# Spreading the last routing over the expert pairs and reordering the step from attention to experts, in a gated cross-attention and mixture-of-experts kernel

## The chip, the cores and the metric

The kernel runs on one core of a Trainium2 chip. The core has a matrix engine (TensorE, PE in the profile, with its weight loads shown as PEld), VectorE (DVE), ScalarE (ACT), GpSimd (POOL) and SyncE (SP), which here issues most of the DMA transfers. Each engine has its own instruction stream and takes it in order; semaphores tie the streams together. The metric is the device time of one execution in microseconds (us).

## The reference

All arithmetic is in fp32. There are 32 sequences of 112 tokens of width 256, each with a context of 375 rows. First, 16-head cross-attention from the normalized tokens to context and tokens together, with a gated residual; then a mixture of 8 experts of width 1024 with the best two chosen for each token, again with a gated residual.

```python
def _L0_xattn_ref(x, latents, ...):          # x: context, latents: tokens
    x, lat = layer_norm(x, ...), layer_norm(latents, ...)
    q = lat @ Wq
    k, v = split(concatenate([x, lat], axis=1) @ Wkv)
    attn = softmax(einsum('bhid,bhjd->bhij', q, k) * scale)
    return (attn @ v) @ Wout

def _L0_ffn_ref(x, gate_w, w1, b1, w2, b2):
    gate_scores = softmax(xf @ gate_w)
    topk_scores, topk_idx = top_k(gate_scores, 2)     # then normalized to sum 1
    h = gelu(einsum('td,edf->etf', xf, w1) + b1[:, None, :])
    y = einsum('etf,efd->etd', h, w2) + b2[:, None, :]
    out = sum over the two experts of topk_scores * y[expert, token]

x = x + tanh(g_xattn) * _L0_xattn_ref(ctx, _layernorm(x), ...)
x = x + tanh(g_ffn) * _L0_ffn_ref(_layernorm(x), ...)
```

The kernel does not compute all experts for all tokens: it sorts token rows by expert into a table in DRAM and computes only the chosen ones.

## The kernel before

The order of the work on each of the five engines is written out by hand: the order in which the program calls its helpers is the order of each engine's stream (`manual_schedule`). A helper call appends to several streams at once.

**Attention** is a loop of `LAST` = 128 steps n. A step handles four heads of one sequence. Its softmax is pipelined: in step n, VectorE transposes step n's weights in blocks of 32 (`turn_blocks`), SyncE sends them to DRAM in four transfers (`send_blocks`) and takes them back in another layout as `exT` (`take_blocks`, 1 MB, in slot h = 1); TensorE computes step n+1's `scores`, VectorE their maxima, ScalarE the exponentials (`exps`), VectorE a reciprocal and ScalarE a scaling by it (`norm`, in slots 1 and 3). `attend(j)` multiplies the weights of steps 2j and 2j+1 with the values; it is called in step 2j+3, and attend(63) stands behind the loop. A step has five slots h = 0 to 4; the lists `slots` and `pe` hold TensorE work for each slot, `dve` work for other engines, `after` transfers issued in slot 1 behind take_blocks. `ps_m` is a ring of four PSUM tiles that nearly all TensorE results go through, so each result needs the tile of four results earlier to have been read.

**Routing.** Every 128 tokens form a slab: `project`, `residual` (which stores the slab to the output and takes its statistics), `normed`, `gate_turn` and `gate_scores`. Slabs are routed in groups (six of four slabs, then slabs 24 and 25, then 26 and 27) by 13 parts r[0] to r[12] of `route_parts`: largest, equal, first, rest, largest, equal, first, apart, counts, places (two TensorE products), gates, slots_of, out_to. The last part puts two scatters per slab into `outgoing`; a scatter is an indirect DMA from GpSimd that writes one slab's rows to one expert each. `locate_early` and `locate_late` then work out from the counts (`counted`, one TensorE product) where each pair of blocks lies; the latter is cut in 11 pieces by its `yield`s.

**Experts.** There are 21 pairs t = 0 to 20 of 2 x 128 rows of one expert, the first 13 (`EARLY`) located after 20 slabs and the other 8 (`LATE`) after all. Pair 0 is computed plainly between the last attention steps (`hidden_plain`, one hidden chunk of 128 at a time, and `second_plain`). Each later pair uses seven products per layer where eight would be plain (`hidden_pair`, `second_pair`), with sums by VectorE and GpSimd. In the loop, iteration t runs hidden_pair(t), fetches pair t+1's first weights (`fetch_first`: a bias and seven transfers; for many pairs they are skipped on the chip when the expert stays the same), turns pair t+1's rows (`turn_rows`, `rows_sums`), does a few pieces of routing from the list `todo`, runs second_pair(t-1), adds its rows to the output from GpSimd (`out_pair`), fetches the second weights (`fetch_second`) and the rows of pair t+3 (`fetch_rows`). Every fetch_rows waits on all scatters issued since the one before (`behind_all`). Expert weights of the first and second layer have one buffer each. Behind the 21 pairs come single blocks (`run`).

Three places that the change and the steps of the prediction touch:

- the list `todo` (from L1627): what is left of the routing of slabs 24 and 25 (counts, places, gates, slots_of, out_to), then that of slabs 26 and 27, then the 11 pieces of locate_late: 38 entries, two of them empty, done six per iteration from t = 1 by `pieces_of(6)`;
- the iteration with t + AHEAD == EARLY, that is t = 10, in which the rest of `todo` and all of `outgoing` are done ahead of fetch_rows(13), the first fetch that needs the late table;
- steps 125 to 127 (`LAST - 3` to `LAST - 1`), where the expert work starts, and the calls between the loop and iteration t = 1.

Of the kernel before, what the change touches and what calls it, by code (L numbers as in the profile page):

```python
# [10 lines left out]
AF = mybir.ActivationFunctionType  # L11
ALU = mybir.AluOpType
# [11 lines left out]
def kernel(  # L24
# [152 lines left out]
    if True:  # L177
# [331 lines left out]
        def norm(n, p):  # L509
            b, i = heads_of(n)[0], heads_of(n)[1][p]  # L510
            rc = soft.tile([P, 2], F32, tag="rc", name=f"rc_{b}_{i}", bufs=4)
            nc.vector.reciprocal(rc, sm.pop((b, i)))  # L512
            for j in range(2):
                t = exs[n % 2][:, :, p, :, j, :]
                nc.scalar.mul(t, t, rc[:, j : j + 1])  # L515

        def turn_blocks(n, p):

# [90 lines left out]
        def normed(i, eng=nc.gpsimd):  # L609
            g, j = group[i]  # L610
            eng.tensor_scalar(
                xr[g][:, j, 0, :D], x1[i], mvx[i][:, 0, 0:1], rsx[i], ALU.subtract, ALU.mult
            )
            soon_.append(lambda: nc.gpsimd.tensor_copy(xr[g][:, j, 1, :D], xr[g][:, j, 0, :D]))
# [291 lines left out]
        def locate_late():  # L906

            has, behind_ = rank, macc  # L910
            nc.vector.tensor_scalar(has, found["ps"], float(P), None, ALU.is_ge)
            nc.vector.tensor_tensor(behind_, found["ps"], eoff, ALU.add)
            nc.vector.scalar_tensor_tensor(behind_, behind_, float(-PADS), has, ALU.add, ALU.mult)
            nc.vector.tensor_scalar(behind_, behind_, float(PADS), None, ALU.add)
            found["behind"] = mp.tile([P, E], I32, name="behindi")
            nc.vector.tensor_copy(found["behind"], behind_)
            yield
            rest = mp.tile([P, E], F32, name="restl")
            nc.vector.tensor_tensor(rest, found.pop("ps"), found["taken"], ALU.subtract)
            full, first = whole_blocks("b", rest, None, 0.0, 2 * P)  # L920
            yield
            taken = taken_of("b", first, full, LATE)
            start = mp.tile([P, E], F32, name="startl")
            nc.vector.tensor_tensor(start, found["start"], taken, ALU.add)
            yield
            yield from located("b", first, found["start"], row2, 2 * P, False)
            yield
            _, first = whole_blocks("c", rest, taken, float(P - 1), P)
            yield
            yield from located("c", first, start, row, P, True)  # L930
            yield
# [139 lines left out]
        def hidden_plain(lo, hi):  # L1071
            if lo == 0:
                hid[0] = found["tiles"].tile([P, NF, 2, P], F32, tag="h", name="h_0")
            for f in range(lo, hi):
                ps = ps_m.tile([P, 2, P], F32, tag="m", name=f"ps_h_0_{f}")
                for k in range(KD):
                    nc.tensor.matmul(
                        ps,
                        lhsT=found["w1"][:, k, f * P : (f + 1) * P],
                        rhs=xsT[0][:, k],  # L1080
                        start=(k == 0),
                        stop=(k == KD - 1),
                    )
                nc.scalar.activation(  # L1084
                    hid[0][:, f], ps, AF.Gelu, bias=bias[0][0][:, f : f + 1]
                )

        def second_plain(b):
            banks.append(banks.pop(0))
            ps = psy[0, b] = banks[-1][:, 0, :D]  # L1090
            for f in range(NF):
                nc.tensor.matmul(
                    ps,
                    lhsT=hid[0][:, f, b, :],
                    rhs=found["w2"][:, f, :],
                    start=(f == 0),
                    stop=(f == NF - 1),
                )

        def add_rows(t, b, y):  # L1100
# [26 lines left out]
                add_rows(t, b, y[:, b])  # L1127


        def hidden_pair(t):  # L1130


            h = hid[t] = found["tiles"].tile([P, NF, 2, P], F32, tag="h", name=f"h_{t}")
            x, v = xsT[t], xt[t]
            H = NF // 2
            h11, h12, h21, h22 = (h[:, i : i + H, b, :] for i in (0, H) for b in range(2))

            def product(n, w, r):
                ps = ps_m.tile([P, H, P], F32, tag="m", name=f"ps_h_{t}_{n}")
                for c in range(H):  # L1140
                    nc.tensor.matmul(
                        ps[:, c, :], lhsT=wt[w][:, c * P : (c + 1) * P], rhs=r, start=True, stop=True
                    )
                return ps

            def gelu(lo):
                for f in range(lo, lo + H):
                    nc.scalar.activation(h[:, f], h[:, f], AF.Gelu, bias=bias[t][0][:, f : f + 1])  # L1148

            add = nc.vector.tensor_tensor  # L1150
            nc.scalar.copy(h11, product(1, "11", x[:, 0, 0]))
            add(h12, product(6, "s2", v[:, 1]), h11, ALU.add)
            add(h21, product(7, "s3", v[:, 2]), h12, ALU.add)
            ps = product(5, "s1", v[:, 0])
            add(h22, ps, h21, ALU.add)
            add(h12, ps, h12, ALU.add)
            add(h21, product(4, "22", v[:, 3]), h21, ALU.add)  # L1157
            gelu(H)
            add(h11, product(2, "12", x[:, 1, 0]), h11, ALU.add)
            add(h12, product(3, "s4", x[:, 1, 1]), h12, ALU.add)  # L1160
            gelu(0)

# [293 lines left out]
        for n in range(LAST):  # L1456
# [121 lines left out]
                found["early"] = ctx.enter_context(tc.tile_pool(name="early", bufs=1, side="right"))  # L1578
                after += [lambda: fetch_rows(0), weights_ahead]
            if n == LAST - 3:  # L1580
                pe[4].append(lambda: turn_rows(0, nc.scalar.copy))
            if n == LAST - 2:

                pe[0].append(lambda: others(ends))
                after.append(lambda: fetch_first(1))
                for h in range(1, 5):
                    pe[h].append(lambda h=h: hidden_plain(h - 1, h))
            if n == LAST - 1:
                after += [lambda: fetch_second(1)]
                after += [lambda t=t: fetch_rows(t) for t in range(2, 1 + AHEAD)]  # L1590
                for h in range(4):
                    pe[h].append(lambda h=h: hidden_plain(h + 4, h + 5))
                pe[4].append(lambda: turn_rows(1))

            if n > 1 and n % 2:
# [1 line left out]
            more = n + 1 < LAST  # L1597
            if more:
                scores(n + 1)
                exps(n + 1, 0)  # L1600
            for h in range(5):
                for unit in slots[h] + pe[h]:
                    unit()
                if h == 4:
                    break
                if h == 1:
                    take_blocks(n)
                    do(after)
                if more and h in (1, 3):
                    norm(n + 1, h // 2)  # L1610
                if more and h == 3:
                    turn_blocks(n + 1, 0)
                then_ = soon_[:]
                del soon_[:]
                do(then_)
                for part in dve[h]:
                    part()

                if outgoing and (h % 2 == 0 or n > LAST - NG):
                    outgoing.pop(0)()  # L1620
                if extra:
                    do(extra.pop(0))
                if more and h == 0:
                    exps(n + 1, 1)


# [1 line left out]
        r, _ = route_parts(g, nc.vector)  # L1628

        todo = [[part] for parts in extra for part in parts]  # L1630
        todo += [[lambda j=j: normed(j, nc.vector), now] for j in (i, i + 1)]
        todo += [[]]
        todo += [[lambda p=p, j=j: p(j)] for j in (i, i + 1) for p in (gate_turn, gate_scores)]
        todo += [[part] for part in r[:9]] + [[]] + [[r[9]]]
        todo.append([lambda: found.update(ps=counted())])
        todo += [[part] for part in r[10:]]
        late = locate_late()
        todo += [[lambda: next(late)]] * 11

        def pieces_of(n):  # L1640
            for _ in range(min(n, len(todo))):
                do(todo.pop(0))
# [2 lines left out]
        for b in range(2):  # L1645
            second_plain(b)
        rows_sums(1)
        hidden_pair(1)
        attend(LAST // 2 - 1)
        for u in range(2):  # L1650
            project(i + u)
# [3 lines left out]
        for t in range(1, PAIRS):  # L1655
            if t > 1:
                hidden_pair(t)
            fetch_first(t + 1)
            turn_rows(t + 1, nc.scalar.copy if t > 1 else None)
            if t + 1 < PAIRS:  # L1660
                rows_sums(t + 1)
            pieces_of(6)
            hidden_sums(t)
            if t > 1:
                second_pair(t - 1)
# [3 lines left out]
                combine(0)  # L1669
                do(found.pop("sums"))  # L1670
            if t + AHEAD == EARLY:
                pieces_of(len(todo))
                do(outgoing)
                del outgoing[:]
            fetch_rows(t + AHEAD)
# [70 lines left out]
```

## Time and profile before

| | |
|---|---|
| three runs | 2023.91, 2027.59 and 2034.03 us, median 2027.59 |
| profiled execution, timed | 2025.86 us |
| its span, first to last instruction | 2024.2 us |
| mean granted TensorE clock | 0.994 |

| stretch of the span, us | TensorE busy | VectorE busy | GpSimd busy | granted clock | DMA share |
|---|---|---|---|---|---|
| 0 to 1540 | 1504.55 | 1134.95 | 743.70 | 1.00 | 0.74 |
| 1540 to 1600 | 50.99 | 23.71 | 14.30 | 0.94 | 0.73 |
| 1600 to 1711 | 100.03 | 78.36 | 78.02 | 0.94 | 0.63 |
| 1711 to 1890 | 174.73 | 91.61 | 129.19 | 1.00 | 0.85 |
| 1890 to 2024 | 122.20 | 19.60 | 29.35 | 0.98 | 0.61 |

The first stretch is attention up to step 123, the second the passage to the experts, the third pairs 2 to 8, the fourth pairs 9 to 20, the last the single blocks. Rows of the timeline merge neighbouring instructions of one line; a row gives the start, the time up to the last one's end, the engine, the line, the operation with output and inputs, the count, and in brackets the idle time of the engine before it with what ended it. `SPq` is SyncE's queue of DMA issues: its durations are those of issuing, not of the transfer. Granted clock is the share of full speed at which TensorE was allowed to run; it is 1.0 or 0.5 at any moment.

### The profile page before, as it was taken

Reading aid. Unit: us, or ns where it says so; the run is one execution under the profiler, and the core shown is the slowest. Engines: PE = TensorE matmul, PEld = TensorE weight load, DVE = VectorE, ACT = ScalarE, POOL = GpSimd, SP = SyncE. Lnnn points to the kernel's source line nnn. Section 1 sums busy time; section 2 is a strip of 40 time slices with the busy share of each in tenths; the row PEclk is TensorE's granted clock in tenths of the full one; section 3 lists DMA queues with packets and bytes.
Section 4 is the critical chain, followed back from the end, with each engine's and each line's share of the span. In section 5 each row is a group of like instructions: output and inputs, shape, how many; then the busy total and the mean of one; then the engine's idle time right before and its main releaser. Section 6 shows DMA issues by size and latency. Waiting matters only on the chain. (4 is left out here: it accounts for less than half of the span.)

```text
span 2024.2 us, 41138 instructions
## 1 busy us (share of the span) xinstructions
PE 1952.5 (96%) x14352; PEld 1494.6 (74%) x14352; DVE 1348.2 (67%) x2417; ACT 1156.5 (57%) x2718; POOL 994.6 (49%) x1469
## 2 busy tenths in 40 slices
PE   8999999999999999999999999999998899999998
PEld 4676767676667677767666676777676799999887
DVE  6777776777786767676777777777776467545111
ACT  5666666656666666566666666666656233334342
POOL 5534243435265745564556555642424367767322
PEclk9999999999999999999999999999999899999999
DMA  7676666667677878788878778876657567799773
GB/s 218 199 224 191 180 193 185 197 167 208 197 233 221 260 216 245 220 262 232 258 211 260 220 239 231 255 222 175 190 166 240 185 194 202 197 324 285 204 210 51
DMA packets 261057, 433.40 MB, mean 214 GB/s; under 512 B 30729, under 2 KB 149073, under 8 KB 244465
## 3 DMA queue, kind: packets, MB, share of 16 engines
q1 hardware_dynamic: 248384, 414.37, 68.6%
q0 software_dynamic: 11328, 15.33, 3.9%
q8 instruction: 115, 1.88, 0.4%
q10 hardware_dynamic: 1136, 1.05, 0.2%
q14 instruction: 94, 0.76, 0.1%
HBM read 301.37 MB, written 172.28 MB: 234 GB/s over the span
## 5 line engine op out<-in xcount | busy, mean ns | idle before, releaser
L501 ACT ACTIVATE ex<-bank,nmx 128x512 f32<-128x512 f32 x512 | 348.7, 689 | 259.7 <-DVE nmx L492 259.7
L515 ACT ACTIVATE ex<-ex,rc 128x512 f32<-128x512 f32 x512 | 342.4, 720 | 202.8 <-DVE rc L512 201.5
L492 DVE TENSOR_REDUCE nmx<-bank 128x2 f32<-128x974 f32 x256 | 286.2, 1158 | 122.6 <-PE bank L482 122.6
L520 DVE STREAM_TRANSPOSE ex<-ex 128x1024 f32<-128x1024 f32 x256 | 315.1, 1231 | 28.4 <-ACT ex L515 25.6
L422 POOL TENSOR_TENSOR kT<-tmpk,kT 128x487 f32<-128x487 f32 x63 | 76.9, 1221 | 388.1 <-ACT kT L440 388.1
L412 PEld LDWEIGHTS ps_v<-wkv_s,tT 128*128 128x128 f32 x1536 | 189.3, 192 | 77.7 <-DVE kT L446 35.7
L482 PE MATMUL bank<-kT,qTs 64*128 64x487 f32 x1024 | 243.7, 594 | 0.0
L546 PE MATMUL ps_o<-exT,vv 128*64 128x112 f32 (+1 forms) x4096 | 211.2, 260 | 1.5 <-ACT h L1084 1.5
L412 PE MATMUL ps_v<-wkv_s,tT 128*128 128x128 f32 x1536 | 199.0, 278 | 11.6 <-DVE kT L446 10.0
L546 PEld LDWEIGHTS ps_o<-exT,vv 128*64 128x64 f32 (+1 forms) x4096 | 197.4, 136 | 9.5 <-ACT h L1084 1.9
L446 DVE TENSOR_TENSOR vv<-ps_v,vv 128x512 f32<-128x512 f32 x192 | 131.9, 687 | 108.4 <-PE ps_v L412 85.9
L406 PE MATMUL ps_k<-tT,wkv_s 128*128 128x487 f32 x378 | 181.0, 583 | 13.9 <-DVE vv L446 13.8
L412 PEld LDWEIGHTS ps_v<-wkv,kvT 128*128 128x128 f32 x1024 | 129.2, 191 | 72.4 <-issue 65.5
L1102 POOL DMA_INDIRECT out_dram<-y,xs x60 | 93.4, 1557 | 168.0 <-DVE y L1126 79.3
L422 POOL TENSOR_TENSOR vv<-tmpv,vv 128x512 f32<-128x512 f32 x64 | 81.5, 1274 | 190.7 <-ACT vv L440 190.6
L482 PEld LDWEIGHTS bank<-kT,qTs 64*128 64x128 f32 x1024 | 88.1, 186 | 103.3 <-issue 92.4
L1330 POOL TENSOR_TENSOR piece<-piece 128x128 f32<-128x128 f32 x256 | 117.3, 458 | 61.5 <-DMA piece<-in_L_ffn_w_dram 41.1
L446 DVE TENSOR_TENSOR kT<-ps_k,kT 128x487 f32<-128x487 f32 x189 | 123.3, 657 | 29.5 <-PE ps_k L406 24.3
L412 PE MATMUL ps_v<-wkv,kvT 128*128 128x128 f32 x1024 | 141.4, 281 | 0.0
L406 PE MATMUL ps_k<-kvT,wkv 128*128 128x487 f32 x252 | 130.2, 598 | 0.0
L333 PE MATMUL ps_q<-kvT,wq_sb 128*128 128x224 f32 x512 | 120.0, 356 | 1.4 <-ACT kvT L321 0.7
L1148 ACT ACTIVATE h<-h,b 128x256 f32<-128x256 f32 x160 | 66.2, 495 | 93.4 <-DVE h L1157 92.8
(297 smaller groups left out, 3683.4 us busy)
## 6 DMA issues: line engine op xcount, KB each, us to landing
turned<-ex SPq DMA_DIRECT2D x512, 256.0 KB
exT<-turned SPq DMA_DIRECT2D x128, 1024.0 KB
w<-in_L_ffn_w_dram SPq DMA_DIRECT2D x132, 256.0 KB
w_s<-ws SPq DMA_DIRECT2D x80, 256.0 KB
w_t<-ws SPq DMA_DIRECT2D x80, 256.0 KB
w_b2x<-in_L_ffn_w_dram SPq DMA_DIRECT2D x38, 512.0 KB
ws<-piece SPq DMA_DIRECT2D x64, 256.0 KB
cin<-in_ctx_dram SPq DMA_DIRECT2D x32, 336.0 KB
```

Of the source, the lines that this page charges most:

```text
L333: nc.tensor.matmul(ps, lhsT=wq_sb[:, k, i * P : (i + 1) * P], rhs=kvT[g][:, k, :, SC:NK], start=(k == 0), stop=(k == KD - 1),)
L406: nc.tensor.matmul(ps, lhsT=w[:, 0, i * P : (i + 1) * P], rhs=x[:, :NK], start=True, stop=True)
L412: nc.tensor.matmul(ps[:, c, :], lhsT=x[:, c * P : (c + 1) * P], rhs=w[:, 1, i * P : (i + 1) * P], start=True, stop=True,)
L422: nc.gpsimd.tensor_tensor(v[o], v[l], v[r], ALU.add)
L446: nc.vector.tensor_tensor(v[at], product(n, w, x), v[at], ALU.add)
L482: nc.tensor.matmul(ps[:, j, :NK], lhsT=qT[b // 2, i][r, b % 2].rearrange("p a i -> p (a i)"), rhs=kT[b, i][r, :], start=True, stop=True,)
L492: nc.vector.tensor_reduce(nmx[b, i], pss[b, i][:, :, :NK], AX.X, ALU.max, negate=True)
L501: nc.scalar.activation(exs[n % 2][:, :, p, :, j, :], ps[:, j, :].rearrange("p (c k r) -> p k c r", c=NCK, r=QW), AF.Exp, bias=nmx[b, i][:, ...
L515: nc.scalar.mul(t, t, rc[:, j : j + 1])
L520: nc.vector.transpose(t, t)
L546: nc.tensor.matmul(ps[y * DH : (y + 1) * DH, r, x * S : (x + 1) * S].rearrange("p (a i) -> p a i", a=QB), lhsT=vv[j][:m, c, x, r, y * DH : ...
L1330: nc.gpsimd.tensor_tensor(o, l, r, op) for o, l, r, op in ops
```

## The change

- **Step 125:** `turn_rows(0)` moves from slot 4 to slot 2.
- **Step 126:** both `exps` of step 127 move from before and in slot 0 to slot 2, both `norm` to slot 3; the scaling in step 127's norm is by VectorE and not by ScalarE. Two chunks of hidden_plain (not four) are computed here, in slots 1 and 2; their results are copied by ScalarE without Gelu. `fetch_rows(2)` and `fetch_rows(3)` come from step 127 to here, ahead of `fetch_first(1)`.
- **Step 127:** six chunks of hidden_plain in slots 0 to 3; the Gelu of chunks 0 and 1 follows those of 6 and 7, and second_plain takes chunks 0 and 1 last.
- **First pair:** up to one left-over routing piece of slabs 24 and 25 in each of six places within hidden_pair(1); then fetch_first(2), turn_rows(2) and rows_sums(2), which come ahead of attend(63) and the last projections and not behind them.
- **Pairs 1 to 13:** 31 pieces in the portions 2, 1, 2, 4, 3, 3, 3, 3, 2, 3, 1, 2, 2; the empty entries go, and where a portion holds a TensorE piece it stands first. `counted` stands behind slots_of and ahead of out_to.
- **t = 10:** the rest of `todo` is no longer done at once; `outgoing` still is.
- In locate_late one subtraction moves from the second piece to the first.

```diff
@@ norm
             for j in range(2):
                 t = exs[n % 2][:, :, p, :, j, :]
-                nc.scalar.mul(t, t, rc[:, j : j + 1])
+                if n == B * NG - 1:
+                    nc.vector.tensor_scalar(t, t, rc[:, j : j + 1], None, ALU.mult)
+                else:
+                    nc.scalar.mul(t, t, rc[:, j : j + 1])
@@ locate_late
-            yield
             rest = mp.tile([P, E], F32, name="restl")
             nc.vector.tensor_tensor(rest, found.pop("ps"), found["taken"], ALU.subtract)
+            yield
@@ hidden_plain
-                nc.scalar.activation(
-                    hid[0][:, f], ps, AF.Gelu, bias=bias[0][0][:, f : f + 1]
-                )
+                if f < 2:
+                    nc.scalar.copy(hid[0][:, f], ps)
+                    continue
+                for f_ in (f, f - 6) if f > 5 else (f,):
+                    nc.scalar.activation(
+                        hid[0][:, f_],
+                        ps if f_ > 1 else hid[0][:, f_],
+                        AF.Gelu,
+                        bias=bias[0][0][:, f_ : f_ + 1],
+                    )
@@ second_plain
-            for f in range(NF):
+            for n in range(NF):
+                f = (n + 2) % NF
...
@@ hidden_pair
-        def hidden_pair(t):
+        def hidden_pair(t, between=lambda: None):
...
             nc.scalar.copy(h11, product(1, "11", x[:, 0, 0]))
+            between()
             add(h12, product(6, "s2", v[:, 1]), h11, ALU.add)
+            between()
             add(h21, product(7, "s3", v[:, 2]), h12, ALU.add)
+            between()
             ps = product(5, "s1", v[:, 0])
             add(h22, ps, h21, ALU.add)
             add(h12, ps, h12, ALU.add)
+            between()
             add(h21, product(4, "22", v[:, 3]), h21, ALU.add)
             gelu(H)
+            between()
             add(h11, product(2, "12", x[:, 1, 0]), h11, ALU.add)
+            between()
             add(h12, product(3, "s4", x[:, 1, 1]), h12, ALU.add)
@@ attention loop
             if n == LAST - 3:
-                pe[4].append(lambda: turn_rows(0, nc.scalar.copy))
+                pe[2].append(lambda: turn_rows(0, nc.scalar.copy))
             if n == LAST - 2:
                 pe[0].append(lambda: others(ends))
+                after += [lambda t=t: fetch_rows(t) for t in range(2, 1 + AHEAD)]
                 after.append(lambda: fetch_first(1))
-                for h in range(1, 5):
+                for h in range(1, 3):
                     pe[h].append(lambda h=h: hidden_plain(h - 1, h))
             if n == LAST - 1:
                 after += [lambda: fetch_second(1)]
-                after += [lambda t=t: fetch_rows(t) for t in range(2, 1 + AHEAD)]
-                for h in range(4):
-                    pe[h].append(lambda h=h: hidden_plain(h + 4, h + 5))
+                for h, lo, hi in ((0, 2, 4), (1, 4, 6), (2, 6, 7), (3, 7, 8)):
+                    pe[h].append(lambda lo=lo, hi=hi: hidden_plain(lo, hi))
                 pe[4].append(lambda: turn_rows(1))
...
                 scores(n + 1)
-                exps(n + 1, 0)
+                if n != LAST - 2:
+                    exps(n + 1, 0)
...
-                if more and h in (1, 3):
+                if n == LAST - 2 and h == 3:
+                    norm(n + 1, 0)
+                if more and h in (1, 3) and (n, h) != (LAST - 2, 1):
                     norm(n + 1, h // 2)
...
-                if more and h == 0:
+                if n == LAST - 2 and h == 2:
+                    exps(n + 1, 0)
+                if more and h == (2 if n == LAST - 2 else 0):
                     exps(n + 1, 1)
@@ behind the attention loop
         todo = [[part] for parts in extra for part in parts]
+        own = -len(todo)
         todo += [[lambda j=j: normed(j, nc.vector), now] for j in (i, i + 1)]
-        todo += [[]]
         todo += [[lambda p=p, j=j: p(j)] for j in (i, i + 1) for p in (gate_turn, gate_scores)]
-        todo += [[part] for part in r[:9]] + [[]] + [[r[9]]]
+        todo += [[part] for part in r[:10]]
+        todo += [[part] for part in r[10:12]]
         todo.append([lambda: found.update(ps=counted())])
-        todo += [[part] for part in r[10:]]
+        todo.append([r[12]])
+        shares = [2, 1, 2, 4, 3, 3, 3, 3, 2, 3, 1, 2, 2]
         late = locate_late()
         todo += [[lambda: next(late)]] * 11
+        own += len(todo)
...
-        hidden_pair(1)
+        hidden_pair(1, lambda: pieces_of(min(1, len(todo) - own)))
+        fetch_first(2)
+        turn_rows(2)
+        rows_sums(2)
         attend(LAST // 2 - 1)
...
             if t > 1:
                 hidden_pair(t)
-            fetch_first(t + 1)
-            turn_rows(t + 1, nc.scalar.copy if t > 1 else None)
-            if t + 1 < PAIRS:
-                rows_sums(t + 1)
-            pieces_of(6)
+                fetch_first(t + 1)
+                turn_rows(t + 1, nc.scalar.copy)
+                if t + 1 < PAIRS:
+                    rows_sums(t + 1)
+            pieces_of(shares.pop(0) if shares else 0)
             hidden_sums(t)
...
             if t + AHEAD == EARLY:
-                pieces_of(len(todo))
                 do(outgoing)
                 del outgoing[:]
             fetch_rows(t + AHEAD)
```

More of the change, by code (lines that the diff above doesn't have):

```diff
@@ L1095, in second_plain @@
                     rhs=found["w2"][:, f, :],
-                    start=(f == 0),
-                    stop=(f == NF - 1),
+                    start=(n == 0),
+                    stop=(n == NF - 1),
                 )
```

## The prediction

> **What bounds the kernel now.** I read the page's busy shares first, then TensorE's own timeline from 1540 us on with the reason in brackets for each gap, then SyncE's and GpSimd's timelines at the places where the change moves a step.
>
> ```profile
> PE 1952.5 (96%) x14352; PEld 1494.6 (74%) x14352; DVE 1348.2 (67%) x2417; ACT 1156.5 (57%) x2718; POOL 994.6 (49%) x1469
> ```
>
> TensorE is busy 96% of the span, so only its gaps, and the stretches at half clock behind them, can be won. The changed code starts at step 125 of 128, near 1544 us. From there:
>
> ```profile
> 1555.37 5.16 PE L1077 MATMUL ps_h<-xsT,w 128*128 128x256 f32 x16 [2.31 <-ACT xsT L1056]
> 1562.07 3.30 PE L546 MATMUL ps_o<-exT,vv 128*64 128x112 f32 x64 [1.53 <-ACT h L1084]
> 1565.30 3.72 PE L1077 MATMUL ps_h<-xsT,w 128*128 128x256 f32 x16
> ...
> 1582.55 3.30 PE L546 MATMUL ps_o<-exT,vv 128*64 128x112 f32 x64
> 1585.78 7.17 PE L583 MATMUL ps_p<-wo_sb,outT 128*128 128x256 f32 x32
> ...
> 1597.37 0.61 PE L694 MATMUL ps_pos<-had,ones 128*128 128x16 f32 x2 [3.85 <-POOL had L686]
> 1598.68 2.05 PE L1141 MATMUL ps_h<-xsT,w 128*128 128x128 f32 x8 [0.71 <-DMA w<-in_L_ffn_w_dram]
> ...
> 1610.58 0.61 PE L630 MATMUL ps_g<-gate_sb,xgT 128*128 128x8 f32 x4 [2.84 <-ACT xgT L625]
> ...
> 1642.85 0.37 PE L693 MATMUL ps_pos<-both,before 128*128 128x16 f32 x2 [2.05 <-DVE both L679]
> ...
> 1689.38 1.16 PE L1141 MATMUL ps_h<-xsT,w 128*128 128x128 f32 x8 [2.82 <-DVE h L1152]
> ```
>
> Columns: start, duration, then in brackets the gap and its releaser. The first row (16 matmuls in 5.16 us) and the third (the same 16 in 3.72) show the second cost of a gap: a slow stretch. Eight matmuls of a pair take 2.05 us at 1598.68 and 1.06 elsewhere. I call the start of pair t's first product Ht. In this trace H1 is 1576.20, H2 1598.68, H3 1621.01, H9 1711.32, H11 1737.20, H12 1750.14. From H9 to H12 a pair takes 12.94; from H3 to H9, six pairs take 90.31, not 77.7.
>
> Two more views, for what the change makes late:
>
> ```profile
> 1569.82 3.57 SPq L526 DMA_DIRECT2D turned<-ex  x4
> 1576.89 0.34 SPq L533 DMA_DIRECT2D exT<-turned  x1
> ```
>
> ```profile
> 1740.18 0.39 SPq L958 DMA_DIRECT2D xs<-xg  x1
> 1741.48 0.33 SPq L978 DMA_DIRECT2D b<-b1d  x1
> 1742.16 0.33 SPq L1017 DMA_DIRECT2D w<-in_L_ffn_w_dram  x1
> ```
>
> ```profile
> 1719.91 1.27 POOL L1181 TENSOR_TENSOR ex<-h,ex 128x512 f32<-128x512 f32 x1
> 1721.34 1.02 POOL L730 DMA_INDIRECT xg<-xr,sloti  x1 [0.15 <-issue]
> ```
>
> The first is the sending and taking of step 127, between attention and experts; the second pair 13's rows, then pair 12's weights, on SyncE; the third the last scatter of routed rows, 10.0 us after H9.
>
> **Part 1, between attention and experts.** turn_rows(0) goes from slot 4 to slot 2 of step 125, so ScalarE copies xsT before the second norm and not after it. The 2.31 gap goes, and the slow stretch behind it (5.16-3.72 = 1.44). Two hidden chunks are copied (nearest row, a 128x256 copy from PSUM: 0.39 each) and their Gelu comes later, so the 1.28 us table load no longer stands in front of attend(62); its 1.53 gap goes too. Step 127's norms move to VectorE: four scalings of 128x512. The nearest rows, 128x256 scalings, took 0.35 alone and 3.77 beside two GpSimd adds; doubled, 0.7 to 7.5 each. GpSimd does under 1.5 us of work from 1556 to 1567, so I take 0.7: transposed by 1565 (1566.5 before), hidden since SyncE sends only later.
>
> That sending is what comes late next. fetch_rows(2) and (3) now stand before pair 1's weights on SyncE, and the four sends queue behind those. The two fetches took 1.42 in the trace (1583.03 to 1584.45). So sends at 1571.2, take at 1578.3, and the 1 MB exT (by the trace's packets it ended 4.1 us after 1576.89) at 1582.5. TensorE, without its gaps: attend(62) at 1556.3 (exT of step 125 ends about 1556.1), +3.24, six chunks 5.36, turn 0.45, second_plain 6.9: pair 1 at 1572.3. Pair 1 takes 6.3 and the two placing products 0.5, turn_rows(2) 0.5: 1579.5. Then it waits 3.1 us for exT, and attend(63) starts at 1582.6, where it did before. Part 1's winnings are lost here; bounds on this wait: 0 (the sends catch up) and 6 (data 3 us later still). A 3.1 gap mostly brings a slow stretch, some 1.0 on average by the 1.44 above.
>
> [...]
>
> **Part 2, from projection to pair 3.** Projections end near 1593.0, plus 1.0. The placing matmuls (3.85 gap) now lie beside pair 1, and pair 2's weights are fetched before residual's stores, so 0.71 goes: H2 = 1594.0, 4.7 earlier. From H2: 12.94, one gate transposition 0.4, and VectorE late by residual(27) 1.2, a root 0.9, normed 0.4, combine(0) 2.7, hence L1152 ends 5.9 after H2 where product 2 wants its buffer at 4.5: 1.4, with followers 2.1. H3 = 1594.0+15.4 = 1609.4 instead of 1621.0: **11.6 won**. The 2.84 gap (its product now a pair after its copy) and 1.65 of slow clock are in it.
>
> **Part 3, pairs 3 to 8.** The pieces' TensorE work remains: 0.75 in pair 3, 0.36 in pair 4, 0.6 in pair 7, 0.3 in pair 8: 2.0. Six pairs then take 77.7+2.0 = 79.7: **10.6 won**. VectorE covers the pieces if they take at most 5.4 us in a pair: it is free from H+8.2 (1676.77 after H6) to H+13.1, less one 0.3 add, and L1152 may be 1.1 late (done at 3.3 after H, wanted at 4.5). In the trace six pieces with 9.2 us of VectorE (1676.77 to 1686.0) broke this and made the 2.82 gap. Now pair 10 has the most, the three located pieces (5.2 in this trace, L836 to L862); others 2 to 3.5. Without that cover the excess goes straight to TensorE.
>
> **Part 4, what the spreading makes late.** out_to, in pair 5 before, is now piece 20 and falls in pair 8 (2+1+2+4+3+3+3 = 18 pieces before it). It makes four scatters; pair 8 and 9 end with one each, and at the end of pair 10 (t+3 = 13 = EARLY) do(outgoing) emits two, directly before fetch_rows(13), which waits for every scatter. In the old order they ended with pair 8 and it waited for nothing. On GpSimd they follow out_pair(9): first at H11+10.0, the second 1.3 later (1553.18 to 1554.50 for such a pair), and the profile's median from scatter to landing is 3.3: H11+14.7. SyncE arrives at H11+3.0 and stands. Behind it: pair 12's weights, then second(11), rows 14, pads. From rows to the first weight is 2.0 (1740.18 to 1742.16), so that weight is issued at H11+16.9 to 17.7; at 1595.66 such a load released TensorE 3.0 later: H11+20.5, wanted at 12.94. **Stall 7.5**, and 1.8 for slow clock (2.0 and 1.65 behind the gaps at 1597 and 1610). Bounds: 0 (scatters early) and 12 (landing 7.7 us, the trace's longest for a weight). Pair 13's weight then follows at 8.9 after pair 12's late start, wanted with 4.9 for landing at 14.6: hidden again. **9.3 lost.**
>
> [...]
>
> **Sum.** 11.6+10.6-9.3 = 12.9 off the span of 2024.2: 2011.3, and with the 1.7 around it (2025.86 timed) **2013**. That run lies 1.7 under the median 2027.59; runs reached from 2023.9 to 2034.0. Past pair 13 the pairs are paced as before, so the tail only shifts.
>
> **Rivals.**
> 1. The scatters are no wait: SyncE finds them landed. Then 22.2 are won: 2003.7. For: before, no fetch of rows shows a wait on one. Against: there each had a whole pair of time.
> 2. The front yields less: exT comes 3 us later since 0.5 MB more rows and weights share the DMA engines, with a full slow stretch (1.7 more), and fetch_rows(13) costs 12 instead of 9.3. 2013+3+1.7+2.7 = 2020.4, about no change. For: the DMA's rate was already 281 to 402 GB/s from 1568 to 1576 (its view in 2 us slices).
> 3. Slower: VectorE's small pieces become the bound. If contention with GpSimd stretches them over 5.4 us in pairs 3 to 10, as 0.17 us operations that took 1.1 to 1.2 (1628.42, 1641.35) and the 3.77 hint, each of eight pairs gets the 2.82 gap: 22.6, so 2035.6. Against: only one pair in this trace passed the limit, with six located pieces.
>
> **Chances.** Forecast 0.52 (2007 to 2019); rival 1 0.16; rival 2 0.20; rival 3 0.12. About 0.5%, 10 us, is what a measurement can tell from no change, so faster means under 2017.4: 0.43 of the forecast, rival 1, and 0.03 of rival 2: 0.62. Same: 0.09+0.17 = 0.26. Slower: 0.12. The range 2001 to 2026 takes in rivals 1 and 2 and leaves out rival 3 and some edges.
>
> **What would show it.** Right: no gaps at the old places; attend(63) waiting on exT near 1582; H3 near 1609, six pairs to H9 in about 80; SyncE's pair 13 rows some 15 us after H11 and a 7 us gap at pair 12 put down to a weight's DMA. Wrong: attend(63) well before 1580; no gap at pair 12; gaps on L1152 in pairs 4 to 10; or new gaps before 1572.

## The result, and the profile after

| | before | after |
|---|---|---|
| median of 7 runs each | 2028.02 us (2023.91 to 2034.03) | 2018.33 us (2015.19 to 2020.37) |
| profiled execution, timed | 2025.86 | 2015.19 |
| its span | 2024.2 | 2013.4 |
| mean granted TensorE clock | 0.994 | 0.998 |

The ratio is 0.9946, with an interval from 0.9931 to 0.9962: 0.38 to 0.69% faster, so the lower end lies under the 0.5% that the prediction set as its bound, and the median over the 2017.4 that it set for faster. 2013 was forecast; the median came out 5.3 us above it and inside the range. The profiled execution of after is the fastest of its seven runs, so the trace shows the change at its best.

Line numbers have moved: the seven products of a pair are L1141 before and L1152 after, VectorE's adds into h L1152 before and L1164 after. The page's busy line first, then TensorE's timeline with the same columns as in the prediction.

```profile
PE 1947.9 (97%) x14352; PEld 1489.3 (74%) x14352; DVE 1352.2 (67%) x2421; ACT 1155.6 (57%) x2716; POOL 995.3 (49%) x1470
```

```profile
1574.34 1.13 PE L1152 MATMUL ps_h<-xsT,w 128*128 128x128 f32 x8 [0.88 <-DMA w<-in_L_ffn_w_dram]
...
1581.64 0.99 PE L549 MATMUL ps_o<-exT,vv 128*64 128x112 f32 x16
1585.69 2.53 PE L549 MATMUL ps_o<-exT,vv 128*64 128x112 f32 x48 [3.06 <-DMA exT<-turned]
1588.15 7.17 PE L586 MATMUL ps_p<-wo_sb,outT 128*128 128x256 f32 x32
1595.16 1.05 PE L1152 MATMUL ps_h<-xsT,w 128*128 128x128 f32 x8
...
1600.74 1.16 PE L1152 MATMUL ps_h<-xsT,w 128*128 128x128 f32 x8 [0.95 <-DVE h L1164]
...
1611.58 1.06 PE L1152 MATMUL ps_h<-xsT,w 128*128 128x128 f32 x8
...
1691.71 1.06 PE L1152 MATMUL ps_h<-xsT,w 128*128 128x128 f32 x8
...
1736.27 2.05 PE L1152 MATMUL ps_h<-xsT,w 128*128 128x128 f32 x8 [5.56 <-DMA w<-in_L_ffn_w_dram]
```

The rows at 1574.34, 1595.16, 1611.58, 1691.71 and 1736.27 are H1, H2, H3, H9 and H12. The gaps of 2.31, 1.53, 3.85, 0.71, 2.84, 2.05 and 2.82 us shown of before have no counterpart. In their place stand a wait of 3.06 inside attend(63), 0.95 on an add at 1600.74, and 5.56 at pair 12. The matmuls that follow the last run at half clock (granted 0.50 from 1734.6 to 1741.4; 2.05 us for eight, not 1.06).

The cause of that gap is on two other queues: GpSimd's scatters, and SyncE's issues for pair 13's rows and pair 12's weights.

```profile
1727.66 1.02 POOL L733 DMA_INDIRECT xg<-xr,sloti  x1 [0.16 <-issue]
1728.98 0.99 POOL L733 DMA_INDIRECT xg<-xr,sloti  x1 [0.19 <-issue]
```

```profile
1719.59 0.34 SPq L984 DMA_DIRECT2D b<-in_L_ffn_b_dram  x1
1731.65 0.39 SPq L961 DMA_DIRECT2D xs<-xg  x1
1732.95 0.33 SPq L981 DMA_DIRECT2D b<-b1d  x1
1733.62 0.33 SPq L1020 DMA_DIRECT2D w<-in_L_ffn_w_dram  x1
```

SyncE issues nothing from 1719.93 to 1731.65, until the scatter of 1728.98 has landed 2.67 us after its start; the trace puts 11.1 us of this down to the scatters. The weight behind it goes at 1733.62, and TensorE starts 2.65 later.

For the wait in attend(63), the sending and taking of step 127 on SyncE:

```profile
1572.96 4.04 SPq L529 DMA_DIRECT2D turned<-ex  x4
1580.84 0.34 SPq L536 DMA_DIRECT2D exT<-turned  x1
```

Put together over the profiled executions, each stretch by TensorE's starts:

| stretch | before | after | won |
|---|---|---|---|
| to H3 | 1621.01 | 1611.58 | 9.4 |
| H3 to H9 | 90.31 | 80.13 | 10.2 |
| H9 to H12 | 38.82 | 44.56 | -5.7 |
| H12 to H18 | 81.47 | 84.23 | -2.8 |
| H18 to the end | 192.6 | 192.9 | -0.3 |
| span | 2024.2 | 2013.4 | 10.8 |

### The profile page after: what moved, and what is told of

It reads as the page before. It is cut to its first block, busy times and chain, and to the rows that moved or that the text cites. A ratio compares the mean times of both kernels' runs of the same rounds, so it can differ in the third digit from the quotient of the medians.

```text
span 2013.4 us, 41135 instructions
## 1 busy us (share of the span) xinstructions
PE 1947.9 (97%) x14352; PEld 1489.3 (74%) x14352; DVE 1352.2 (67%) x2421; ACT 1155.6 (57%) x2716; POOL 995.3 (49%) x1470
## 5 line engine op out<-in xcount | busy, mean ns | idle before, releaser
L412 PE MATMUL ps_v<-wkv_s,tT 128*128 128x128 f32 x1536 | 199.0, 278 | 11.6 <-DVE kT L446 10.0
```

The source lines that it names most:

```text
L412: nc.tensor.matmul(ps[:, c, :], lhsT=x[:, c * P : (c + 1) * P], rhs=w[:, 1, i * P : (i + 1) * P], start=True, stop=True,)
```

## The experiments

The theory: the change wins in the passage and in pairs 2 to 8 what gaps and half clock cost before, and gives part of it back at two waits, for exT in attend(63) and for the scatters ahead of pair 13's rows. Main rivals: the wait at pair 12 is something else that would stay, or the new order in the passage is worth more, or less, than the prediction says.

**Scatters two at a time.** After, with pairs 8 and 9 ending in two scatters each, so that none is left for pair 10.

```diff
-            if outgoing:
+            for _ in range(min(len(outgoing), 2 if t in (8, 9) else 1)):
                 outgoing.pop(0)()
```

> The changed kernel, but pairs 8 and 9 end with two scatters each, so that none is left to be issued ahead of pair 13's rows. Theory (SyncE stands at pair 13's rows until two scatters have landed, and pair 12's weights queue behind it): the 5.56 us gap ahead of pair 12 falls under 0.6 and the half clock behind it goes, about 8 us less than the changed kernel, ratio to the kernel before 0.991. Rival (pair 12's weights are late by themselves, because the DMA engines are busy there): a gap of 4 us or more stays, ratio 0.9946 as for the change.

Measured: 2008.3 us, ratio 0.9904 [0.9889, 0.9919]. TensorE at pair 12, then SyncE at the same place:

```profile
1733.45 1.06 PE L1215 MATMUL bank<-w_b2x,ex 128*128 128x128 f32 x8
1734.35 1.06 PE L1152 MATMUL ps_h<-xsT,w 128*128 128x128 f32 x8
```

```profile
1724.14 0.39 SPq L961 DMA_DIRECT2D xs<-xg  x1
1725.43 0.33 SPq L981 DMA_DIRECT2D b<-b1d  x1
1726.11 0.33 SPq L1020 DMA_DIRECT2D w<-in_L_ffn_w_dram  x1
```

And the last scatter, on GpSimd:

```profile
1719.96 0.98 POOL L733 DMA_INDIRECT xg<-xr,sloti  x1 [0.19 <-issue]
```

No bracket at 1734.35, and eight matmuls take 1.06 again. The last scatter starts at 1719.96, 9.0 us ahead of after's and a pair before anyone waits for it; the weight is issued 8.2 us before it is used, not 2.65. The wait for scatters is shown as the cause of the gap and of the half clock behind it. The routing alone, which also leaves two scatters for pair 10, has this gap too, of 6.90 us. The version is faster than both kernels; the intervals do not overlap.

**The passage alone.** Before, with after's steps 125 to 127 and nothing of the routing's new spreading (hidden_pair without places for pieces, six pieces at the end of each pair, fetch_first(2) and turn_rows(2) behind the projections). The main lines, against after:

```diff
-        hidden_pair(1, lambda: pieces_of(min(1, len(todo) - own)))
-        fetch_first(2)
-        turn_rows(2)
-        rows_sums(2)
+        hidden_pair(1)
...
-            pieces_of(shares.pop(0) if shares else 0)
+            pieces_of(6)
```

> The kernel before with the change's steps 125 to 127 alone (order between attention and experts), its routing pieces left as they were. Theory (what these steps win on TensorE is lost again while attend(63) waits for step 127's data, which come later): a gap of 2 to 4 us inside attend(63), projections end 0 to 2 us later than before, ratio 1.000 (0.999 to 1.001). Rival (they win what their gaps held, some 4 us): ratio 0.998 or less.

Measured: 2031.75, ratio 1.0015 [1.0006, 1.0024]. Inside attend(63):

```profile
1583.66 4.75 PE L549 MATMUL ps_o<-exT,vv 128*64 128x112 f32 x48 [4.53 <-DMA exT<-turned]
```

Slightly slower than before: the wait is 4.53 here, and the 48 matmuls take 4.75 us (2.53 above), at a granted clock of 0.50 from 1582.16 to 1589.00. Wait, end of the projections (2.9 us later than before) and ratio all lie a little above the theory's ranges. Pair 1 starts at 1571.71, 4.5 us earlier than before; by themselves the new steps win nothing, since what they save comes back at exT.

**The routing alone.** After, with the old steps 125 to 127, where the rows of pairs 2 and 3 are fetched behind pair 1's second weights. Of the edit, only the lines on these rows are shown:

```diff
             if n == LAST - 2:
-                after += [lambda t=t: fetch_rows(t) for t in range(2, 1 + AHEAD)]
                 after.append(lambda: fetch_first(1))
...
             if n == LAST - 1:
                 after += [lambda: fetch_second(1)]
+                after += [lambda t=t: fetch_rows(t) for t in range(2, 1 + AHEAD)]
```

> The changed kernel with steps 125 to 127 as they were before, so the routing part of the change alone. Theory (the whole gain is in the routing part): at least as fast as the whole change, ratio 0.994, with no wait inside attend(63). Rival (the two parts add up, some 4 us from steps 125 to 127): ratio 0.9965.

Measured: 2024.34, ratio 0.9975 [0.9964, 0.9986]. The theory's 0.994 lies outside; the rival's 0.9965 lies within the interval, but for a reason that is not the rival's. TensorE, then SyncE:

```profile
1588.97 1.08 PE L1052 MATMUL ps_x<-ident,xs 128*128 128x128 f32 x4 [6.08 <-DMA xs<-xg]
```

```profile
1578.77 2.54 SPq L1034 DMA_DIRECT2D w_t<-ws  x4
1581.50 0.33 SPq L981 DMA_DIRECT2D b<-in_L_ffn_b_dram  x1
1582.35 1.28 SPq L958 DMA_DIRECT2D xs<-xg  x2
```

attend(63) has no wait for exT, as the theory had it. The lost time is a wait that neither had named: turn_rows(2) now stands ahead of attend(63), and with the old order its rows are issued at 1582.35 only. Moving turn_rows(2) forward and fetching its rows earlier belong together.

**The routing, and the rows ahead.** The previous kernel, with fetch_rows(2) and (3) put ahead of fetch_second(1) in step 127.

```diff
             if n == LAST - 1:
+                after += [lambda t=t: fetch_rows(t) for t in range(2, 1 + AHEAD)]
                 after += [lambda: fetch_second(1)]
-                after += [lambda t=t: fetch_rows(t) for t in range(2, 1 + AHEAD)]
```

> As e3 (the routing part of the change with the old steps 125 to 127), but in step 127 the rows of pairs 2 and 3 are fetched ahead of pair 1's second weights and not behind them. Theory (e3 lost because turn_rows(2), now ahead of attend(63), met rows that were fetched too late, and not because it lacked the rest of the new steps): the 6.08 us wait for rows goes and the half clock with it, ratio 0.9945 (0.993 to 0.9955), as good as the whole change. Rival (the rest of steps 125 to 127 brings 4 us or more): ratio 0.9965 or more.

Measured: 2017.19, ratio 0.9943 [0.9929, 0.9956], as after's 0.9946.

```profile
1584.55 0.63 PE L1052 MATMUL ps_x<-ident,xs 128*128 128x128 f32 x4 [0.38 <-DMA xs<-xg]
1585.11 3.30 PE L546 MATMUL ps_o<-exT,vv 128*64 128x112 f32 x64
1588.34 7.17 PE L583 MATMUL ps_p<-wo_sb,outT 128*128 128x256 f32 x32
1595.35 1.05 PE L1141 MATMUL ps_h<-xsT,w 128*128 128x128 f32 x8
```

The 6.08 is 0.38, attend(63) runs through, and H2 is 1595.35 against after's 1595.16. So of all edits in steps 125 to 127 only the rows' place is worth time here; the rest (turn_rows(0) earlier, the chunks without Gelu, VectorE's scalings) is worth nothing measurable, since the 3.5 us by which TensorE reaches attend(63) earlier in after (1581.64 for 1585.11) are spent in its wait of 3.06 for exT.

**Sends first.** After, with step 127's sends ahead of pair 1's weights.

```diff
             if n == LAST - 2:
-                after += [lambda t=t: fetch_rows(t) for t in range(2, 1 + AHEAD)]
-                after.append(lambda: fetch_first(1))
...
             if n == LAST - 1:
-                after += [lambda: fetch_second(1)]
+                pe[0].append(lambda: fetch_first(1))
+                pe[0].append(lambda: fetch_rows(2))
+                after += [lambda: fetch_second(1), lambda: fetch_rows(3)]
```

> The changed kernel, but SyncE issues step 127's four sends ahead of pair 1's weights and of the rows of pairs 2 and 3. Theory (attend(63) waits because the sends queue on SyncE behind those transfers): the wait inside attend(63) falls from 3.06 to under 0.5, pair 1's weights come later and may hold it for up to 2 us, net 2 to 3.5 us less than the changed kernel, ratio 0.993. Rival (the DMA engines are full from 1566 to 1586 whatever the order): the waits only change places, ratio 0.9946 as for the change.

Measured: 2014.09, ratio 0.9933 [0.9919, 0.9946].

```profile
1576.04 1.13 PE L1152 MATMUL ps_h<-xsT,w 128*128 128x128 f32 x8 [2.81 <-DMA w<-in_L_ffn_w_dram]
...
1583.34 3.30 PE L549 MATMUL ps_o<-exT,vv 128*64 128x112 f32 x64
...
1593.59 1.05 PE L1152 MATMUL ps_h<-xsT,w 128*128 128x128 f32 x8
```

The wait for exT is gone, and the one for pair 1's weights is 2.81 instead of 0.88. So most of the wait moved to what is issued last, as the rival had it, but not all: the two waits sum to 2.81 for 3.94, H2 is 1.6 us earlier than in after, and the ratio is the theory's 0.993 (its interval and after's overlap).

**Weights first, with two scatters.** To see whether only SyncE's order makes one of the two late: pair 1's weights ahead of step 126's take, then step 127's sends, pair 2's rows, the take, the second weights, pair 3's rows.

```diff
+                pe[0].append(lambda: fetch_first(1))
...
-                after += [lambda t=t: fetch_rows(t) for t in range(2, 1 + AHEAD)]
-                after.append(lambda: fetch_first(1))
...
-                after += [lambda: fetch_second(1)]
+                pe[0].append(lambda: fetch_rows(2))
+                after += [lambda: fetch_second(1), lambda: fetch_rows(3)]
...
```

> The changed kernel with two scatters at the end of pairs 8 and 9 (as in e1) and another order on SyncE: pair 1's weights go out ahead of the taking of step 126, in the time in which SyncE stands for the sends of step 126 to land; then the sends of step 127, then the rows of pair 2, the taking of step 127, second weights, the rows of pair 3. Theory (both waits at the passage come from SyncE's order): the gap ahead of pair 1 and the one inside attend(63) fall under 0.5 each, 4 to 7 us less than e1, ratio 0.9875. Rival (the DMA engines are full there whatever the order): one of the waits stays at 2 us or more, ratio 0.9895 or more.

Measured: 2007.75, ratio 0.9895 [0.9878, 0.9911], as the rival had it, and within noise of the kernel with two scatters. The trace is of an execution of 2010.74, the second longest of five. TensorE, SyncE, then the view of the DMA engines from 1566 to 1582 in 40 slices of 0.4 us (busy tenths, and GB/s):

```profile
1573.24 1.05 PE L1152 MATMUL ps_h<-xsT,w 128*128 128x128 f32 x8
...
1583.94 4.16 PE L549 MATMUL ps_o<-exT,vv 128*64 128x112 f32 x48 [2.48 <-DMA exT<-turned]
```

```profile
1568.88 2.24 SPq L529 DMA_DIRECT2D turned<-ex  x4
1572.02 0.41 SPq L961 DMA_DIRECT2D xs<-xg  x1
1579.01 0.34 SPq L536 DMA_DIRECT2D exT<-turned  x1
```

```profile
DMA  8998989899998969968989999999982000096599
GB/s 277 369 410 318 241 230 266 297 343 384 348 399 318 317 230 348 287 246 348 425 328 364 399 405 399 410 405 400 370 283 104 21 21 0 0 164 184 246 471 430
```

The weights are in time (no bracket at 1573.24), and the sends are out at 1571.1, 5.9 earlier than in after, where they ended at 1577.0. Yet the take follows at 1579.0 and not at 1580.8: it wins 1.8 of 5.9. The engines were busy throughout until 1578.0 or so; the sends seem to have landed when that backlog was worked off. In after the same view, over 1566 to 1584 in slices of 0.45 us, ends its block at about 1579.0:

```profile
DMA  9499999999959799998999999999951001091889
GB/s 200 164 382 400 437 400 366 313 372 368 314 169 229 218 323 346 401 355 319 387 332 373 405 419 396 410 396 405 369 209 46 18 0 36 0 328 18 364 364 437
```

From 1572 to 1576 the engines' mean busy share is 0.99 in after and 0.98 in the run with the weights first. So in this passage weights, rows and sends seem to compete for bytes, not only for places on SyncE, and which of them waits is a choice. That one of them must wait is not shown: two of the five executions took 2004.14 and 2004.20, the time that the theory gave, at a granted clock of 0.999 (0.997 in the traced one), and they were not profiled. Nor was it tried to move some bytes elsewhere. The row of after has 396 to 419 GB/s in its fullest stretch of several slices; single slices lie above that (437 there, 471 in the run with the weights first).

**Placing behind counting.** After, with one more piece in pair 6 and one less in pair 7, so that the placing products stand in pair 6 at the back of the pieces that they need.

```diff
-        shares = [2, 1, 2, 4, 3, 3, 3, 3, 2, 3, 1, 2, 2]
+        shares = [2, 1, 2, 4, 3, 4, 2, 3, 2, 3, 1, 2, 2]
```

> The changed kernel with the portions of pairs 6 and 7 four and two in place of three and three, so that the placing products stand right behind counts in pair 6 and not first in pair 7. Theory (the gaps came from TensorE meeting a product whose input VectorE makes in the same pair): a gap of 2 us ahead of the first placing product and one of 0.9 ahead of the second, and some half clock behind them, as at 1642.85 in the kernel before. Rival (VectorE is early enough in this order): no gap over 0.3.

One run, too few for a ratio: 2020.74 us. The trace answers:

```profile
1662.22 0.37 PE L696 MATMUL ps_pos<-both,before 128*128 128x16 f32 x2 [2.05 <-DVE both L682]
1663.49 0.40 PE L697 MATMUL ps_pos<-had,ones 128*128 128x16 f32 x2 [0.91 <-DVE had L689]
1663.74 1.63 PE L1215 MATMUL bank<-w_b,h 128*128 128x128 f32 x8
```

The 2.05 of before is back to the hundredth, with 0.91 behind it and a slow stretch (1.63 us for eight matmuls, not 1.06). In after the same matmul stood at the head of its portion, a pair later than VectorE's work, without a bracket (1671.85). From H3 to H9 this run took 85.44, 5.3 more than after. So that TensorE's pieces come first and a pair after their operands is about half of the 10.2 won in Part 3.

**Five late pieces in one pair.** After, with pair 9 given five pieces and pair 10 none.

```diff
-        shares = [2, 1, 2, 4, 3, 3, 3, 3, 2, 3, 1, 2, 2]
+        shares = [2, 1, 2, 4, 3, 3, 3, 3, 5, 0, 1, 2, 2]
```

> The changed kernel with five of locate_late's pieces in pair 9 (the second to the sixth) and none in pair 10. They took 8.6 us of VectorE in the trace of before. Theory (up to 5.4 us a pair are covered, the excess goes to TensorE): a gap of about 3.2 us in pair 10, ahead of its sixth product, put down to VectorE's first sum. Rival (other slack covers it): no gap over 0.5 there.

One run: 2018.48 us. The trace again, TensorE, and the first and last of VectorE's pieces:

```profile
1711.60 1.16 PE L1152 MATMUL ps_h<-xsT,w 128*128 128x128 f32 x8 [1.54 <-DVE h L1164]
```

```profile
1699.69 1.31 DVE L819 TENSOR_SCALAR wholeb<-restl 128x8 int32<-128x8 f32 x1
...
1708.12 0.17 DVE L865 CAST whereib<-whereb 128x4 int32<-128x4 f32 x1
```

The excess goes straight to TensorE, as the prediction had it, though at half the size expected: 1.77 us (1.54, and 0.23 on the next add). The pieces took 8.6 us in this pair (1699.69 to 1708.29), so 6.8 of them were hidden, not 5.4. VectorE began them 7.2 us after the pair's start (1692.48 in this run), where the prediction had 8.2. The terms that stand in the prediction for the 5.4 (13.1 less 8.2, less 0.3, plus 1.1) add up to 5.7; with the start 1.0 earlier they give 6.7.

## Why the prediction was right, and where it was off

The mechanisms came out as written, and the sum was close: against the profiled execution 12.9 was forecast and 10.8 came, and the medians are 9.7 apart. The traced stretches differ from the forecast by -2.2 (to H3), -0.4, +0.8 and, in the tail, -0.3. That the profiled 2015.19 lies so near to 2013 is in part luck, since it is the fastest of seven executions.

- **Part 1: the wait was right in kind, its size by luck.** attend(63) was to wait 3.1 for exT and waited 3.06. But both sides came about 3 us later than forecast. TensorE began attend(63) at 1581.64 (1579.5 forecast) and did 16 of its 64 matmuls before it met the wait, and exT came at 1585.69 (1582.5). Of TensorE's delay 1.37 is from attention before any changed step (attend(61) began at 1540.51, 1539.13 before, and from 1538.68 to 1540.46 in the other kernels, whose code up to there is the same) and 0.88 is a wait for pair 1's weights, which the prediction did not have. SyncE's sends began at 1572.96 (1571.2), 1.8 late; from there to the take it was 7.9 for 7.1, and from the take to the data 4.8 for 4.2. The prediction argued from SyncE's order alone; the run with the weights first, where sends issued 5.9 earlier brought the take only 1.8 earlier, speaks for the DMA engines' load (0.98 busy there from 1572 to 1576) counting as well. The slow stretch of 1.0 on average did not come in this execution.
- **The size of that wait varies.** Other kernels with the same steps had 5.81 (two scatters), 3.89 (placing behind counting), 4.03 (five late pieces) and 4.53 (the passage alone), and in all four the 48 matmuls behind it took 3.69 to 4.75 us for 2.53, in the passage alone at a granted clock of 0.50. This is the mechanism of rival 2, and a likely part of why the other six runs of after took longer than its profiled one. Their granted clock, 0.995 to 0.996 for 0.998, fits; they were not profiled, so it is not shown.
- **Part 2: 9.4 won instead of 11.6.** H2 was 1595.16 (1594.0 forecast). What set it was exT, 3.2 later than forecast, less about 0.8 for the 16 matmuls already done and less the slow stretch of 1.0 that did not come. H2 to H3 took 16.42 (15.4): VectorE was late as foreseen, by 0.95 and 0.23 at its adds, and smaller waits for GpSimd's sums of 0.47 and 0.19 came with it. All three gaps named are gone.
- **Part 3: right to 0.4 us.** 80.13 for six pairs (79.7). Rival 3 fell: TensorE idled 0.15 us in all from H3 to H9 and not at all from there to the gap at pair 12, and the run with five pieces shows that the bound exists but lies at 6.8 us of pieces, 1.4 above the prediction's.
- **Part 4: right mechanism, its main term too large.** The gap is 5.56 for 7.5, and the stretch to H12 lost 5.7. The terms that stand there (10.0, 1.3, 3.3 and 2.0) put the weight's issue at H11+16.6, but 17.5 was used (20.5 less 3.0); nothing there gives the rest. It went at H11+16.0 (1733.62 less 1717.60), for 1.5 of the difference. The scatter's landing, 2.67 for 3.3, is 0.6 of that. The 3.3 was the median of four scatters of the passage; that of all 56 before is 4.9, from 2.5 to 7.7, so this one was quick. (The 7.7 of the upper bound is the longest of a scatter and not of a weight.) From weight to product it was 2.65 for 3.0. The half clock cost more than the 1.8: pair 12 took 15.47, 2.53 over 12.94. Part 4 lost 8.5 for 9.3.
- **Rival 1 named what was to be had**: 2003.7 without the wait at the scatters; the kernel with two scatters took 2008.3, with the 5.81 wait in its profiled run.

## What to carry to other kernels

A step moved out of the way takes its data with it: for each moved step, follow what the next in-order queue behind it still has to issue, and whether that step's own inputs are fetched in time at the new place (out_to's scatters here, and the rows for turn_rows(2)). Emptying a list "at the end" ahead of a fetch that waits for all of it puts the whole landing time on the queue (SyncE stood 11.1 us for the scatters in after); sending two a turn in the last two turns took the ratio from 0.9946 to 0.9904. Where the DMA engines were full, as in the passage here, reordering the issues mostly chose which consumer waited: 0.88 and 3.06 us in after, 2.81 at pair 1 with the sends first, 2.48 at exT with the weights first. That fewer or earlier bytes would remove the wait was not tried.

## What was not expected of the hardware

- **A gap of 3.06 us cost no clock, while 2.05 and 0.91 together did.** In after the granted clock was 1.00 from 1581 to 1588, around the 3.06 gap. In before, 2.05 and 0.91 were followed by 6.83 us at a granted clock of 0.50 (from 1643.7); in the run with placing behind counting, by eight matmuls in 1.63 us, not 1.06. Of the other gaps over 1.5 us between 1500 and 1700 of before, 2.31 and 2.84 were each followed by 3.41 us at 0.50 (from 1554.9 and 1612.9) and 3.85 by 6.83 (from 1595.9), while behind 1.53 and 2.82 it stayed at 1.00 (1560 to 1566 and 1686 to 1700). In after, 5.56 was followed by 6.83 us at 0.50 (from 1734.6). So 2.31 cost clock at one place, and 2.82 and 3.06 did not at others: in these traces the length of a gap alone did not tell what followed, and what else decides is not shown.
- **A send's landing time said little on its own.** Four sends of 256 KB took 3.8 us from the last issue to the take in after, and 7.9 in the run with the weights first, both times issued while the engines were full. In after they were issued later, when less of the backlog was left ahead of them; that this is the reason fits both views and was not tested by itself.
